# Another order of the first stage's steps and loads in a fused cross-attention and mixture-of-experts block

## The chip, the cores and the metric

The kernel runs on one core of one Trainium2 chip. A core has five engines with instruction queues of their own: TensorE (PE in the profile; PEld is its loading of weights), VectorE (DVE), ScalarE (ACT), GpSimd (POOL) and SyncE (SP), which here issues most of the DMA transfers. The metric is the device time of one execution in microseconds; smaller is better. Before the change the median of three runs was 314.81 us (314.62 to 315.84).

## The reference

The block adds two branches to x (2 x 512 rows of 1024). The first multiplies two matrices that are quantized to 8 bits and back; the second is a mixture of experts with one shared and two chosen experts per row.

```python
def fake_quant(x, scale, zp):
    q = jnp.clip(jnp.round(x / s + z), 0.0, 255.0)
    return (q - z) * s

def _L0_xattn_ref(x1, x2, x1_scale, x1_zp, x2_scale, x2_zp):
    return jnp.matmul(fake_quant(x1, x1_scale, x1_zp), fake_quant(x2, x2_scale, x2_zp))

def _L0_ffn_ref(x, router_w, ...):
    scores = softmax(xt @ router_w + router_b) + router_bias
    # 16 experts in 4 groups: the best 2 of the best 2 groups are chosen, gate holds their scores
    ...
    for each expert:  h = silu(xt @ w1 + b1) * (xt @ w2 + b2);  y += gate * (h @ w3 + b3)
    z = silu(xt @ sw1 + sb1) * (xt @ sw2 + sb2) @ sw3 + sb3       # shared expert, 512 wide
    return y + z

x = x + tanh(g_xattn) * _L0_xattn_ref(_layernorm(x), ctx_4096, ...)
x = x + tanh(g_ffn) * _L0_ffn_ref(_layernorm(x), ...)
```

## The kernel before

The 1024 rows are eight tiles X0 to X7 of 128 rows; tiles 0 to 3 belong to batch 0, 4 to 7 to batch 1. The context of a batch is 1024 x 1024, read as eight tiles c.0 to c.7 of 128 rows.

The kernel has a first stage, in which both quantized products, the second normalization and the first part of the shared expert are worked out, and later stages of dense matmuls (the rest of the shared expert, the router, the chosen experts, the down projections), in which the order of the work is written in loops and lists further down. This change touches the first stage alone. Its order is written out by hand in the string START (line 43): each word is a step, and a line of code (760) calls the function of that name, in that order, under a manual schedule. A step's instructions go to the queue of the engine that it names, so the order of the words is the order on each engine, and an engine that waits holds up everything behind it in its queue. The waits for data and for buffers follow from the tiles that the steps read and write.

The steps, by their letters; t is a row tile, b a batch, k a context tile, h a half of the columns, c a chunk of the shared expert (128 of its 512 columns), i its first or second weight:

- bn, ag (184, 188): statistics of tile t, for the first normalization, on VectorE; each half takes 512 columns.
- qa, qp, qr (193 to 202): variance plus epsilon, the power -1/2 (always on GpSimd), and the scale and offset that join normalization and quantization. qn (206) turns the offset's sign, for ScalarE's form.
- q8 (216, or 214 on ScalarE): tile t to 8-bit numbers. qc (169 on ScalarE, 171 otherwise): minus the zero point, to bf16. qt (227): eight transposes on TensorE. qe (163, 165): the transposed tile from PSUM to SBUF.
- c8 (240, 242) and cc (169, 171): the same two conversions for a context tile.
- mm.t.k (252): two matmuls of 512 columns that add context tile k to tile t's product. The whole sum over k stays in two PSUM banks.
- e (264): X = X + scaled product, with the row sums. sq (273), fm, fc, fa, fr (282 to 298), fn (302): the second normalization. px (307): four transposes; xh and xl (163, 317): the transposed rows as a high and a low part. xc (324): a negated copy for the router, in batch 1.
- wh, wl (163, 165 and 555): the same split for a half of a shared weight. um.c.lo.i.p (564): pass p of three (high x high, high x low, low x high) of chunk c for 256 rows of batch 0; us and ug (571, 574) finish it, ud (331) stores it.
- kb.n (536): n matmuls of zeros, which nobody reads, to keep TensorE at work. xd (328): stores X for the last stage. ld (576): the loads of batch 1's context and of X6 and X7. lw (582): the router's weights. lv (587): both weights of chunk 2; lz: those of chunk 3. pb, bt: the biases, transposed. stage, xx: take buffers. pw (616): the sum of XH and XL for the router, four adds of 128 x 1024 on GpSimd (642). rc (601): constants of the router.

The first loads are not in START, but in LOADS (line 42), issued before it on SP's queue in that order (lines 496 to 507): x.t a row tile, c.k a context tile of batch 0 (c.7 in halves), w.c.i a shared weight, b the biases. X0 is loaded ahead of all, in two halves. Eight transfers are under way at a time: each waits until the eighth before it has landed.

Buffers: six PSUM banks for products (ps_mm) and two for transposes (ps_tr), seven small buffers for the 8-bit and bf16 tiles, 14 of 16 KB per partition (octs) and 17 of 4 KB (slabs). A step that takes a buffer waits until its last reader is done.

After START the rest of the shared expert begins with L364, for batch 1 (from 94.42 us), then the router (L653, from 99.88 us).

Of the kernel before, what the change touches and what calls it, by code (L numbers as in the profile page):

```python
# [42 lines left out]
START = """
bn.0.0 bn.0.1 kb.12 ag.0 qa.0.dve kb.1 bn.1.0 bn.1.1 kb.3 ag.1 qp.0 qr.0.pool qa.1.pool stage.0 kb.2 q8.0.dve.0 bn.3.0
qp.1 bn.3.1 qc.0.act.0 c8.0.0.act.0 ag.3 ld qt.0.0 qr.1.pool qa.3.pool q8.1.dve kb.3 q8.0.dve.1 qp.3 qr.3.pool
qe.0.act.0 c8.0.0.dve.1 kb.3 cc.0.0.pool.0 q8.3.dve qc.1.act cc.0.0.pool.1 c8.0.1.act cc.0.1.act qt.1 qc.0.act.1
qe.1.dve mm.0.0 bn.2.0 qc.3.pool mm.1.0 bn.2.1 ag.2 qt.3 c8.0.3.act c8.0.2.pool qa.2.pool mm.1.1 qe.3.dve mm.0.1 qp.2
cc.0.2.dve c8.0.4.dve qr.2.pool qt.0.1 cc.0.3.act c8.0.5.act cc.0.4.pool mm.3.0 mm.3.1 mm.0.2 mm.1.2 qe.0.act.1 mm.3.2
c8.0.7.act.0 mm.0.3 q8.2.dve mm.1.3 qc.2.dve cc.0.5.pool mm.3.3 c8.0.6.dve mm.1.4 c8.0.7.pool.1 cc.0.6.dve mm.3.4
mm.0.4 cc.0.7.dve.0 qt.2 lw mm.1.5 mm.1.6 mm.1.7.0 cc.0.7.dve.1 qe.2.act e.1.0 mm.0.5 mm.1.7.1 wh.1.1.0.act e.1.1  # L50
mm.0.6 mm.0.7.0 mm.3.5 mm.0.7.1 e.0.0 mm.3.6 e.0.1 sq.1.0 sq.1.1 fm.1.pool fc.1.pool mm.2.0 bn.4.0 fa.1.dve bn.4.1
fm.0.pool sq.0.0 fr.1 fc.0.dve mm.2.1 pb fn.1.0 mm.2.2 mm.2.3 mm.2.4 sq.0.1 fa.0.pool bt wh.1.0.0.act wh.1.1.1.act
fr.0 mm.2.5 px.1.0.m xx.0 xh.1.0.act fn.1.1 xd.1 px.1.1.m xh.1.1.act fn.0.0 fn.0.1 xd.0 wl.1.0.0.pool ag.4 mm.3.7.0
px.0.0 px.0.1 xl.1.0 xl.1.1 xh.0.0.act mm.2.6 xh.0.1.act mm.3.7.1 mm.2.7.1 xl.0.0 mm.2.7.0 wh.1.0.1.act xl.0.1
qa.4.dve wl.1.1.1.pool wl.1.0.1.pool um.1.0.1.0 bn.5.0 qp.4 qr.4.pool bn.5.1 e.2.0 ag.5 wh.0.0.0.act wh.0.0.1.act
um.1.0.0.0 c8.1.1.pool qn.4.dve stage.1 wh.0.1.0.act e.3.0 wh.0.1.1.act c8.1.0.act qa.5.dve q8.4.act um.1.0.0.1
um.1.0.0.2 qp.5 wl.1.1.0.dve qr.5.dve um.1.0.1.1 wl.0.0.1.dve cc.1.0.act um.0.0.0.0 um.0.0.1.0 um.1.0.1.2
wl.0.0.0.pool um.0.0.1.1 lv us.1.0 q8.5.dve um.0.0.0.1 qc.4.act wl.0.1.0.dve c8.1.2.pool qt.4 qc.5.act wl.0.1.1.dve
qe.4.act um.0.0.0.2 qt.5 us.0.0 cc.1.1.pool ug.1.0 ud.1.0 um.0.0.1.2 e.2.1 cc.1.2.act c8.1.5.act c8.1.3.pool qe.5.dve
mm.4.0 mm.5.0 cc.1.3.pool cc.1.5.act c8.1.4.dve ug.0.0 ud.0.0 c8.1.6.dve bn.6.0 cc.1.4.pool mm.4.1 c8.1.7.pool  # L60
cc.1.6.act mm.4.2 sq.2.0 mm.5.1 wh.2.0.0.act cc.1.7.pool bn.6.1 mm.4.3 bn.7.0 bn.7.1 sq.2.1 mm.5.2 mm.4.4 ag.6 ag.7
qa.7.pool wh.2.0.1.dve e.3.1 qp.7 mm.5.3 wl.2.0.1.pool qr.7.dve mm.5.4 qa.6.dve mm.5.5 qn.7.dve q8.7.act mm.4.5
wh.2.1.0.dve qp.6 mm.5.6 qc.7.act mm.4.6 mm.4.7 mm.5.7 um.2.0.0.0 fm.2.pool qr.6.pool wh.2.1.1.dve fc.2.pool fm.3.pool
e.5.0 sq.3.0 fa.2.pool um.2.0.0.1 wl.2.0.0.dve um.2.0.1.0 e.4.0 um.2.0.1.1 qt.7 fc.3.pool sq.3.1 sq.5.0 qe.7.dve
um.2.0.0.2 q8.6.dve e.5.1 mm.7.0 fr.2 mm.7.1 wl.2.1.1.dve mm.7.2 wl.2.1.0.pool mm.7.3 mm.7.4 fa.3.pool mm.7.5 qc.6.act
mm.7.6 fr.3 qt.6 sq.5.1 mm.7.7 fm.5.pool um.2.0.1.2 fc.5.pool fa.5.pool fn.2.0 qe.6.act e.4.1 fn.2.1 xd.2 us.2.0 fr.5
px.2.0.m e.7.0 mm.6.0 fn.3.1 px.2.1 sq.4.0 e.7.1 xh.2.0.act fm.4.pool mm.6.1 mm.6.2 ug.2.0 ud.2.0 sq.7.0 mm.6.3 mm.6.4
mm.6.5 fn.3.0 xd.3 px.3.0.m px.3.1 mm.6.6 sq.4.1 fn.5.1 xh.2.1.act mm.6.7 fm.7.pool xl.2.0 xh.3.0.act xx.1 fn.5.0 xd.5
xh.3.1.act rc fc.4.dve xl.2.1 fa.4.pool sq.7.1 xl.3.0 e.6.0 px.5.1.m sq.6.0 um.2.256.1.0 xl.3.1 um.1.256.0.0 e.6.1
um.2.256.0.0 fm.6.dve fc.7.pool fa.7.pool fc.6.dve fr.7 sq.6.1 fa.6.pool px.5.0 um.1.256.0.1 fn.7.0 xh.5.1.act xc.5.1  # L70
fr.4 um.1.256.0.2 fn.7.1 xd.7 fr.6 fn.4.0 fn.6.1 xh.5.0.act xc.5.0 um.2.256.0.1 um.2.256.0.2 px.7.0.m fn.4.1 xd.4
px.7.1 xl.5.0 um.1.256.1.0 xh.7.1.dve xc.7.1 um.2.256.1.1 xl.7.1 px.4.0 fn.6.0 xd.6 px.6.1 us.2.256 um.2.256.1.2
px.4.1.m xl.5.1 us.1.256 um.0.256.0.0 xh.7.0.dve xc.7.0 ug.2.256 xh.6.1.act xc.6.1 xh.4.1.act xc.4.1 xl.4.1
um.0.256.1.0 um.1.256.1.1 xl.7.0 xh.4.0.dve xc.4.0 xl.4.0 xl.6.1 px.6.0.m um.1.256.1.2 um.0.256.0.1 ug.1.256
xh.6.0.act xc.6.0 xl.6.0 um.0.256.0.2 um.0.256.1.1 um.0.256.1.2 us.0.256 ug.0.256 lz pw ud.2.256 ud.1.256 ud.0.256
"""


# [1138 lines left out]
```

## Time and profile before

| | us |
|---|---|
| median of three runs (lowest, highest) | 314.81 (314.62, 315.84) |
| the profiled execution | 315.13 |
| its span, from the first to the last instruction | 313.0 |
| TensorE busy | 297.2 |
| VectorE busy | 215.2 |
| ScalarE busy | 144.7 |
| GpSimd busy | 97.9 |
| mean granted TensorE clock | 0.994 of full speed |

The lines that follow under the prediction are from the page of this execution and from answers of its trace. The page cuts the span into 40 slices and gives the busy share of each in tenths. A row of the trace's order of time gives start, duration, engine, source line, operation, output and input, and in brackets the time that the engine had been idle and what released it. VectorE and GpSimd rows of one operation differ in length from case to case, since a duration holds the time in which the instruction stood at its engine.

### The profile page before, as it was taken

The numbers are of one execution on the slowest core, as the hardware profiler recorded it, in microseconds if no ns is written. First come the engines' busy times: TensorE is split into PE (matmuls) and PEld (weight loads), VectorE is DVE, ScalarE is ACT, GpSimd is POOL, SyncE is SP. The second block draws the span as 40 slices with busy tenths as digits, with TensorE's granted clock in tenths as the row PEclk, the third lists the DMA queues.
The fourth block names the chain that finished last, engine by engine and source line by source line (L and its number), as shares of the span: only waits on it lengthen the run. The fifth ranks groups of instructions, "written<-read, shape, count | busy, mean of one in ns | idle before, by whom it ended". The sixth has DMA issues, their size and how long they took to land.

```text
span 313.0 us, 4306 instructions
## 1 busy us (share of the span) xinstructions
PE 297.2 (95%) x1536; PEld 235.7 (75%) x1541; DVE 215.2 (69%) x351; ACT 144.7 (46%) x210; POOL 97.9 (31%) x133
## 2 busy tenths in 40 slices
PE   7488799999999999999999999999999999999993
...
GB/s 196 420 385 338 417 355 150 6 2 342 146 17 37 101 201 214 91 138 30 111 167 33 171 1 168 101 66 325 331 294 346 309 221 287 321 89 73 98 101 73
DMA packets 39838, 56.90 MB, mean 182 GB/s; under 512 B 5547, under 2 KB 23027, under 8 KB 39810
## 3 DMA queue, kind: packets, MB, share of 16 engines
...
## 4 chain that ended last, share of the span: by engine, by line
PE 87%; DMA 6%; SPq 5%; DVE 1%; issue 1%; DVEq 0%
PE sp L564 11%; PE sp L364 11%; PE pb L945 11%; PE pa L945 7%; PE pc L945 6%; DMA cr<-in_dram 6%; PE at L252 5%; PE b7B L408 3%; PE b6B L408 3%; PE b5B L408 3%; PE b4B L408 3%; PE b3B L408 3%; PE px L307 2%; PE b7C L408 2%; PE b7A L408 2%; PE b6C L408 2%
## 5 line engine op out<-in xcount | busy, mean ns | idle before, releaser
L252 PE MATMUL at<-cq,qT 128*128 128x512 bf16 x123 | 29.7, 379 | 2.6 <-POOL cq L171 1.4
L252 PEld LDWEIGHTS <-qT 128*128 128x128 bf16 x128 | 12.2, 98 | 15.4 <-issue 2.8
L798 POOL DMA_DIRECT2D xf<-xf x8 | 7.2, 936 | 27.6 <-PE pl L653 14.7
L916 POOL DMA_DIRECT2D rS<-hrouted x6 | 7.3, 1579 | 23.1 <-DMA rS<-hshared 15.4
L564 PE MATMUL sp<-XH,sb 128*128 128x256 f32 x96 | 14.1, 292 | 0.0
L956 DVE SCALAR_TENSOR_TENSOR Y<-pb,tg,Y 128x512 f32<-128x512 f32 x12 | 8.9, 745 | 7.1 <-PE pb L945 5.5
L564 PE MATMUL sp<-XH,sa 128*128 128x256 f32 x96 | 13.7, 287 | 0.0
L317 DVE TENSOR_TENSOR XL<-px,XH 128x512 fp32r<-128x512 f32 x16 | 10.4, 678 | 3.8 <-ACT xf L324 3.8
L956 DVE SCALAR_TENSOR_TENSOR Y<-pc,tg,Y 128x512 f32<-128x512 f32 x8 | 5.9, 749 | 10.0 <-PE pc L945 10.0
L564 PEld LDWEIGHTS sp<-XH,sb 128*128 128x128 f32 x96 | 12.3, 190 | 0.5 <-DVE sb L165 0.2
L564 PEld LDWEIGHTS sp<-XH,sa 128*128 128x128 f32 x96 | 12.3, 191 | 0.1
L273 ACT ACTIVATE xn<-X,s 128x512 f32<-128x512 f32 x16 | 11.4, 716 | 2.1 <-DVE X L264 1.8
L184 DVE BATCH_NORM_STATS2 st<-X 128x6 f32<-128x512 f32 x16 | 10.3, 680 | 2.9 <-DMA X<-in_dram 2.9
L364 PE MATMUL sp<-XH,sb 128*128 128x512 f32 x48 | 12.2, 396 | 0.0
L302 DVE TENSOR_SCALAR xn<-X,nm,d 128x512 f32<-128x512 f32 x16 | 11.2, 726 | 1.4 <-POOL d L298 1.3
L364 PE MATMUL sp<-XH,sa 128*128 128x512 f32 x48 | 11.9, 390 | 0.0
L169 ACT ACTIVATE qx<-q8x,nz 128x1024 bf16<-128x1024 uint8 (+1 forms) x7 | 7.2, 1023 | 10.1 <-DVE q8x L216 10.0
L264 DVE SCALAR_TENSOR_TENSOR X<-at,cx_scale,X 128x512 f32<-128x512 f32 x16 | 11.6, 740 | 0.1
L307 PE MATMUL px<-ident,xn 128*128 128x128 f32 x64 | 9.2, 274 | 1.9 <-DVE xn L302 1.1
L364 PEld LDWEIGHTS sp<-XH,sb 128*128 128x128 f32 x48 | 8.9, 188 | 2.6 <-issue 0.8
L171 POOL TENSOR_SCALAR cq<-q8c,nz 128x1024 bf16<-128x1024 uint8 (+1 forms) x8 | 10.0, 1251 | 1.1 <-DVE q8c L242 0.7
L364 PEld LDWEIGHTS sp<-XH,sa 128*128 128x128 f32 x48 | 8.9, 188 | 1.8
...
## 6 DMA issues: line engine op xcount, KB each, us to landing
...
```

Of the source, the lines that this page charges most:

```text
L184: nc.vector.bn_stats(st_[t][:, h, :], X[t][:, half(h)])
L252: nc.tensor.matmul(acc[t][h], qT[b][:, t % TB, k, :], cq[b][k // KH][:, k % KH, half(h)], start=(k == 0), stop=(k == KD - 1))
L264: nc.vector.scalar_tensor_tensor(xs, acc[t][h], cx_scale, xs, ALU.mult, ALU.add, accum_out=sq_[t][0][:, h : h + 1])
L273: nc.scalar.activation(xn_[t][:, half(h)], X[t][:, half(h)], AF.Square, bias=s[:, h : h + 1], scale=-float(H), accum_out=q[:, h : h + 1],)
L302: nc.vector.tensor_scalar(xn_[t][:, half(h)], X[t][:, half(h)], nm, r, ALU.add, ALU.mult)
L307: nc.tensor.transpose(px_[t, q][:, k, :], xn_[t][:, ts(4 * q + k, P)], ident)
L317: nc.vector.tensor_tensor(XL[b][q][p], px_[t, q], XH[b][q][p].bitcast(F32), ALU.subtract)
L364: nc.tensor.matmul(p, wx[:, k, :], xx[b][k // KH][:, k % KH, cols], start=first and k == 0, stop=last and k == KD - 1,)
L408: nc.tensor.matmul(p, w[:, k, :], x[:, k, :], start=f and k == 0, stop=l and k == KH - 1, skip_group_check=not first,)
L564: nc.tensor.matmul(up_[c, lo, i], w[:, k, :], x[0][k // KH][:, k % KH, lo : lo + 256], start=p == 0 and k == 0, stop=p == 2 and k == KD - 1,)
L945: nc.tensor.matmul(p, x[:, ts(t, P)], w[:, cl], start=first and k == 0 and i == 0, stop=k == KH - 1 and i == 2, skip_group_check=not first,)
L956: nc.vector.scalar_tensor_tensor(X[t][:, cl], p, tgf, X[t][:, cl], ALU.mult, ALU.add)
```

## The change

The text of both strings is replaced. The number of words of START is 430 in both, and its steps are the same but for the engine that a step names and for which steps are cut into halves. No code below the strings changes.

Conversions by engine in START (a half counts 0.5), before and after: context c8 on ScalarE 6 and 12, VectorE 4.5 and 1.5, GpSimd 5.5 and 2.5; context cc on ScalarE 6 and 6, VectorE 3 and 4.5, GpSimd 7 and 5.5; row tiles qc on ScalarE 6 and 2.5, VectorE 1 and 1, GpSimd 1 and 4.5; qe on ScalarE 4 and 2.5, VectorE 4 and 5.5; weights wh on ScalarE 9 and 6, VectorE 3 and 6; wl on VectorE 6 and 4, GpSimd 6 and 8.

In LOADS, x.4 goes ahead of c.7's second half and x.5 right behind it, and w.0.0 becomes the first of the weights. In START, tile 0's whole scale and its first quantized half come ahead of tile 1's statistics; ld comes later in the list and lv, lw and xd change places; the order of um, of mm for batch 1 and of px for the later tiles changes.

The diff, with the first part of START, up to the middle of batch 1's products:

```diff
-LOADS = "x.1 x.3 c.0 c.1 x.2 c.2 c.3 c.4 c.5 c.6 c.7.0 c.7.1 w.1.1 x.4 b w.1.0 w.0.1 x.5 w.0.0"
+LOADS = "x.1 x.3 c.0 c.1 x.2 c.2 c.3 c.4 c.5 c.6 c.7.0 x.4 c.7.1 x.5 w.0.0 w.1.0 w.1.1 b w.0.1"
 START = """
-bn.0.0 bn.0.1 kb.12 ag.0 qa.0.dve kb.1 bn.1.0 bn.1.1 kb.3 ag.1 qp.0 qr.0.pool qa.1.pool stage.0 kb.2 q8.0.dve.0 bn.3.0
-qp.1 bn.3.1 qc.0.act.0 c8.0.0.act.0 ag.3 ld qt.0.0 qr.1.pool qa.3.pool q8.1.dve kb.3 q8.0.dve.1 qp.3 qr.3.pool
-qe.0.act.0 c8.0.0.dve.1 kb.3 cc.0.0.pool.0 q8.3.dve qc.1.act cc.0.0.pool.1 c8.0.1.act cc.0.1.act qt.1 qc.0.act.1
-qe.1.dve mm.0.0 bn.2.0 qc.3.pool mm.1.0 bn.2.1 ag.2 qt.3 c8.0.3.act c8.0.2.pool qa.2.pool mm.1.1 qe.3.dve mm.0.1 qp.2
-cc.0.2.dve c8.0.4.dve qr.2.pool qt.0.1 cc.0.3.act c8.0.5.act cc.0.4.pool mm.3.0 mm.3.1 mm.0.2 mm.1.2 qe.0.act.1 mm.3.2
-c8.0.7.act.0 mm.0.3 q8.2.dve mm.1.3 qc.2.dve cc.0.5.pool mm.3.3 c8.0.6.dve mm.1.4 c8.0.7.pool.1 cc.0.6.dve mm.3.4
-mm.0.4 cc.0.7.dve.0 qt.2 lw mm.1.5 mm.1.6 mm.1.7.0 cc.0.7.dve.1 qe.2.act e.1.0 mm.0.5 mm.1.7.1 wh.1.1.0.act e.1.1
-mm.0.6 mm.0.7.0 mm.3.5 mm.0.7.1 e.0.0 mm.3.6 e.0.1 sq.1.0 sq.1.1 fm.1.pool fc.1.pool mm.2.0 bn.4.0 fa.1.dve bn.4.1
-fm.0.pool sq.0.0 fr.1 fc.0.dve mm.2.1 pb fn.1.0 mm.2.2 mm.2.3 mm.2.4 sq.0.1 fa.0.pool bt wh.1.0.0.act wh.1.1.1.act
-fr.0 mm.2.5 px.1.0.m xx.0 xh.1.0.act fn.1.1 xd.1 px.1.1.m xh.1.1.act fn.0.0 fn.0.1 xd.0 wl.1.0.0.pool ag.4 mm.3.7.0
-px.0.0 px.0.1 xl.1.0 xl.1.1 xh.0.0.act mm.2.6 xh.0.1.act mm.3.7.1 mm.2.7.1 xl.0.0 mm.2.7.0 wh.1.0.1.act xl.0.1
-qa.4.dve wl.1.1.1.pool wl.1.0.1.pool um.1.0.1.0 bn.5.0 qp.4 qr.4.pool bn.5.1 e.2.0 ag.5 wh.0.0.0.act wh.0.0.1.act
-um.1.0.0.0 c8.1.1.pool qn.4.dve stage.1 wh.0.1.0.act e.3.0 wh.0.1.1.act c8.1.0.act qa.5.dve q8.4.act um.1.0.0.1
-um.1.0.0.2 qp.5 wl.1.1.0.dve qr.5.dve um.1.0.1.1 wl.0.0.1.dve cc.1.0.act um.0.0.0.0 um.0.0.1.0 um.1.0.1.2
-wl.0.0.0.pool um.0.0.1.1 lv us.1.0 q8.5.dve um.0.0.0.1 qc.4.act wl.0.1.0.dve c8.1.2.pool qt.4 qc.5.act wl.0.1.1.dve
-qe.4.act um.0.0.0.2 qt.5 us.0.0 cc.1.1.pool ug.1.0 ud.1.0 um.0.0.1.2 e.2.1 cc.1.2.act c8.1.5.act c8.1.3.pool qe.5.dve
-mm.4.0 mm.5.0 cc.1.3.pool cc.1.5.act c8.1.4.dve ug.0.0 ud.0.0 c8.1.6.dve bn.6.0 cc.1.4.pool mm.4.1 c8.1.7.pool
-cc.1.6.act mm.4.2 sq.2.0 mm.5.1 wh.2.0.0.act cc.1.7.pool bn.6.1 mm.4.3 bn.7.0 bn.7.1 sq.2.1 mm.5.2 mm.4.4 ag.6 ag.7
-qa.7.pool wh.2.0.1.dve e.3.1 qp.7 mm.5.3 wl.2.0.1.pool qr.7.dve mm.5.4 qa.6.dve mm.5.5 qn.7.dve q8.7.act mm.4.5
-wh.2.1.0.dve qp.6 mm.5.6 qc.7.act mm.4.6 mm.4.7 mm.5.7 um.2.0.0.0 fm.2.pool qr.6.pool wh.2.1.1.dve fc.2.pool fm.3.pool
...
+bn.0.0 bn.0.1 ag.0 qa.0.dve qp.0 qr.0.dve q8.0.dve.0 bn.1.0 kb.12 qc.0.pool.0 bn.1.1 stage.0 kb.1 kb.3 q8.0.dve.1 ag.1
+qt.0.0 qe.0.act.0 qa.1.pool bn.3.0 bn.3.1 qc.0.act.1 kb.2 c8.0.0.act.0 c8.0.0.act.1 ag.3 c8.0.1.act qp.1 qa.3.pool
+qp.3 cc.0.1.act xx.0 qr.1.dve cc.0.0.dve.0 c8.0.2.act kb.3 q8.1.dve qr.3.pool cc.0.0.dve.1 mm.0.0 qc.1.dve qt.1
+q8.3.dve qc.3.pool c8.0.3.act kb.3 mm.0.1 qe.1.dve bn.2.0 mm.1.0 bn.2.1 qt.0.1 ag.2 qt.3 qe.3.dve qa.2.dve cc.0.2.pool
+c8.0.4.act qe.0.dve.1 cc.0.4.act mm.1.1 mm.1.2 cc.0.3.pool mm.0.2 c8.0.5.dve cc.0.5.dve mm.3.0 mm.1.3 qp.2 mm.0.3
+qr.2.dve c8.0.7.dve.0 mm.3.1 q8.2.dve cc.0.7.dve.0 mm.1.4 mm.1.5 bn.4.0 mm.0.4 mm.3.2 c8.0.6.act qc.2.pool mm.3.3
+bn.4.1 c8.0.7.pool.1 cc.0.6.act ag.4 mm.1.6 mm.3.4 qt.2 bn.5.0 cc.0.7.pool.1 mm.1.7.0 mm.0.5 mm.0.6 mm.3.5 mm.1.7.1
+qa.4.pool e.1.0 mm.3.6 qe.2.act bn.5.1 qp.4 e.1.1 wh.0.0.0.act mm.0.7.0 sq.1.0 mm.0.7.1 e.0.0 sq.1.1 e.0.1 ag.5
+wl.0.0.0.pool fm.1.pool fc.1.pool mm.2.0 fa.1.dve fr.1 mm.2.1 sq.0.0 mm.2.2 fm.0.dve wh.1.0.0.dve sq.0.1 mm.2.3 mm.2.4
+fc.0.dve fn.1.1 pb fa.0.dve wh.1.1.0.dve mm.2.5 qr.4.pool mm.2.6 px.1.1.m bt wh.0.0.1.act fn.1.0 fr.0 mm.3.7.1
+qa.5.dve ld qp.5 xh.1.1.act mm.2.7.0 px.1.0.m wl.1.0.0.pool fn.0.0 fn.0.1 px.0.0 xl.1.1 px.0.1 mm.3.7.0 e.2.0
+xh.1.0.act mm.2.7.1 xh.0.0.act xh.0.1.act qn.4.dve wh.1.0.1.act wh.1.1.1.dve e.2.1 xl.1.0 wh.0.1.0.act wh.0.1.1.act
+qr.5.pool um.0.0.0.0 um.1.0.0.0 um.0.0.1.0 wl.1.1.1.pool q8.4.act c8.1.1.act xl.0.0 xl.0.1 um.1.0.1.0 wl.1.1.0.pool
+c8.1.5.act q8.5.dve qc.5.pool wl.0.1.1.pool qc.4.act c8.1.2.act wl.1.0.1.dve um.0.0.1.1 lv um.1.0.0.1 wl.0.1.0.dve
+um.0.0.0.1 sq.2.0 qt.5 c8.1.0.pool um.1.0.0.2 e.3.0 wl.0.0.1.dve e.3.1 c8.1.7.act bn.6.0 stage.1 um.0.0.0.2 qe.5.dve
+cc.1.1.act us.1.0 um.0.0.1.2 cc.1.0.pool us.0.0 qt.4 c8.1.4.act um.1.0.1.1 xd.1 qe.4.dve xd.0 um.1.0.1.2 mm.4.0 mm.4.1
+mm.5.0 bn.6.1 mm.5.1 cc.1.2.pool fm.3.pool bn.7.0 mm.4.2 c8.1.3.pool bn.7.1 ag.6 wh.2.1.0.dve wh.2.0.0.dve
+wh.2.0.1.act cc.1.3.act ug.0.0 ug.1.0 c8.1.6.act qa.6.dve wh.2.1.1.dve cc.1.4.pool mm.5.2 ag.7 cc.1.5.dve fm.2.pool
+cc.1.6.act qa.7.dve mm.4.3 sq.3.0 fc.2.pool wl.2.0.0.pool sq.2.1 sq.3.1 mm.5.3 qp.6 cc.1.7.dve mm.4.4 fa.2.dve
+um.2.0.0.0 mm.5.4 mm.5.5 mm.4.5 mm.4.6 qr.6.dve qp.7 qr.7.pool fc.3.pool q8.6.dve mm.5.6 qn.7.dve mm.5.7 fa.3.dve fr.2
+um.2.0.0.1 e.5.0 fn.2.0 fn.2.1 um.2.0.1.0 q8.7.act qc.6.pool mm.4.7 qt.6 um.2.0.1.1 e.4.0 xd.3 qc.7.act qt.7 qe.6.dve
+mm.6.0 e.5.1 mm.6.1 mm.6.2 qe.7.act mm.6.3 mm.6.4 mm.6.5 sq.4.0 sq.5.0 px.2.1 fm.5.dve fr.3 e.4.1 xh.2.1.act fn.3.0
...
```

More of the change, by code (lines that the diff above doesn't have):

```diff
@@ L62 @@
-qa.7.pool wh.2.0.1.dve e.3.1 qp.7 mm.5.3 wl.2.0.1.pool qr.7.dve mm.5.4 qa.6.dve mm.5.5 qn.7.dve q8.7.act mm.4.5
-wh.2.1.0.dve qp.6 mm.5.6 qc.7.act mm.4.6 mm.4.7 mm.5.7 um.2.0.0.0 fm.2.pool qr.6.pool wh.2.1.1.dve fc.2.pool fm.3.pool
-e.5.0 sq.3.0 fa.2.pool um.2.0.0.1 wl.2.0.0.dve um.2.0.1.0 e.4.0 um.2.0.1.1 qt.7 fc.3.pool sq.3.1 sq.5.0 qe.7.dve
-um.2.0.0.2 q8.6.dve e.5.1 mm.7.0 fr.2 mm.7.1 wl.2.1.1.dve mm.7.2 wl.2.1.0.pool mm.7.3 mm.7.4 fa.3.pool mm.7.5 qc.6.act
-mm.7.6 fr.3 qt.6 sq.5.1 mm.7.7 fm.5.pool um.2.0.1.2 fc.5.pool fa.5.pool fn.2.0 qe.6.act e.4.1 fn.2.1 xd.2 us.2.0 fr.5
@@ L67 @@
[L67 to L75, printed above, removed]
+bn.0.0 bn.0.1 ag.0 qa.0.dve qp.0 qr.0.dve q8.0.dve.0 bn.1.0 kb.12 qc.0.pool.0 bn.1.1 stage.0 kb.1 kb.3 q8.0.dve.1 ag.1
```

10 lines of the change are left out of this document (added).

## The prediction, made before the changed kernel ran

> **What bounds the kernel now.** I read the page first (shares and slices), then TensorE's waits, then the order of time in the first 51 us, then stretches of 1 us for the clock.
>
> ```profile
> span 313.0 us, 4306 instructions
> PE 297.2 (95%) x1536; PEld 235.7 (75%) x1541; DVE 215.2 (69%) x351; ACT 144.7 (46%) x210; POOL 97.9 (31%) x133
> PE   7488799999999999999999999999999999999993
> ```
>
> TensorE (PE) is busy 297.2 of 313.0 us; all its holes but the last lie in the first five slices of 7.8 us. After that nothing but its own work sets the time, so the change can win at most holes before 38 us, and loses if it opens new ones later.
>
> ```profile
> PE pq L227 <- ACT qx L169: 4.4, 1, 4.4
> PE at L252 <- POOL cq L171: 1.4, 3, 0.6
> PE px L307 <- DVE xn L302: 1.1, 1, 1.1
> PE at L252 <- DVE cq L171: 0.9, 1, 0.9
> PE px L307 <- DVE mv L188: 0.8, 1, 0.8
> PE pq L227 <- POOL qx L171: 0.4, 1, 0.4
> ```
>
> All waits of TensorE after its start (total, times, longest): 9.0 us. A first one for tile 0's quantized half, then conversions, then the normalized rows before the transposes of L307.
>
> ```profile
> 9.03 1.29 DVE L184 BATCH_NORM_STATS2 st<-X 128x6 f32<-128x512 f32 x2 [2.45 <-DMA X<-in_dram]
> 10.47 0.49 DVE L216 TENSOR_SCALAR q8x<-X,qa,qb 128x512 uint8<-128x512 f32 x1
> 11.00 0.72 ACT L169 ACTIVATE qx<-q8x,nz 128x512 bf16<-128x512 uint8 x1 [6.93 <-DVE q8x L216]
> ...
> 33.44 1.27 POOL L555 TENSOR_TENSOR sa<-sa1r,sa 128x512 fp32r<-128x512 f32 x1
> 33.51 2.89 DVE L302 TENSOR_SCALAR xn<-X,nm,d 128x512 f32<-128x512 f32 x2 [0.45 <-POOL d L298]
> ...
> 37.90 1.30 PE L564 MATMUL sp<-XH,sb 128*128 128x256 f32 x8
> ...
> 50.84 6.85 PE L252 MATMUL at<-cq,qT 128*128 128x512 bf16 x31
> ```
>
> Start, duration, engine, line. Tile 0's scale was ready at 8.0 (L202 on GpSimd, 7.61 + 0.39), but its first half (L216) stands behind tile 1's statistics, which wait for tile 1's load until 9.03. The two L302 at 33.51 took 2.89 where the pair before took 1.00: each ran only when GpSimd's L555 had ended. From 37.90 the shared experts' matmuls (um) run without a hole; mm.4 follows at 50.84.
>
> ```profile
> 12.00:13.00 1.00, 1.00 (x7) 0.58 1.00 410
> 13.00:14.00 1.00, 1.00 (x4) 0.50 1.06 434
> 14.00:15.00 1.00, 1.00 (x7) 0.50 0.99 406
> 15.00:16.00 1.00, 0.59 (x6) 0.72 1.06 434
> 16.00:17.00 1.00, 0.56 (x2) 1.00 1.01 414
> ```
>
> Stretch, sum, TensorE's busy time, granted clock, DMA share, GB/s: half a clock from about 12.0 to 15.4, after the hole of 4.4 us.
>
> **The change, part by part.** No instruction of the main path is added or removed in kind; they change engine and order. I walk the new order (as the built instructions stand, with the producers they wait for) with durations of the trace.
>
> *Tile 0 alone.* The power on GpSimd ends at 7.23. The two scale operations now follow on VectorE (0.15 and 0.27, as L201 and L202 take there at best, 7.75), the first half of q8 0.49 (8.25), its centring on GpSimd 0.57 (the half cq of L171 that released TensorE at 16.14, once VectorE's L216 was out at 15.6): 8.9 instead of 11.72. Transposes 9.4, copy by ScalarE 0.56: 10.0. Nothing follows at once, for mm.0.0 needs the first context tile.
>
> *VectorE* from tile 1's landing at 9.03: statistics 1.29, tile 0's second half 0.49, aggregate 0.2, tile 3's statistics 1.28 and aggregate 0.2 (12.5), tile 1's scale 0.4, half cq 0.45, q8.1 0.81, half cq 0.45, qc.1 0.76: 15.4. So mm.0.0 runs at 13.4 and 14.8 instead of 16.14, but tile 1's transposes come at 15.5, 0.9 later than now (14.56).
>
> *ScalarE* takes six of eight context conversions of batch 0 instead of four: from 10.9, qc 0.72, c8.0 in halves 2 x 0.70, c8.1 1.24 and cc.1 1.06 (spacings of 14.41 to 16.72) make 15.3; c8.2, c8.3, c8.4 19.0, cc.4 20.1, then c8.6 behind its load. The loads keep just ahead: SP's issues at 15.26 and 16.47, each held until an earlier transfer landed, put c.2 at 15.2 and c.3 at 16.4; at 1.25 each c.6 lands at 20.3, so c8.6 is 21.6 and cc.6 22.6. GpSimd: qc.3 17.4, cc.2 18.5, cc.3 19.6 (1.11 each, L171). VectorE again: qe.1, tile 2's statistics, qe.3, half qe.0, c8.5 and cc.5 21.6, halves c8.7 and cc.7 24.0. Now the same tiles 4 to 7 are ready at 23.6, 25.2, 26.5 and 27.7; then at 20.1, 21.6, 22.6 and 24.0 (its second half by GpSimd, after qc.2, 26.6). This is the real gain. x.4 goes ahead of c.7.1 and costs that half 1.25 us: 22.8, hidden, as GpSimd takes it at 24.7; if GpSimd were early, it would wait there.
>
> *TensorE* from 15.5: 28 transposes at 0.056 (0.45 for eight), three fillers, 58 matmuls at 0.215 (16 in 3.62 is 0.226; 6.50 for 32 from 50.84 is 0.203) is 14.9: 30.4 without a wait. Waits: qe.3 for mm.3.0, qc.2, mm.1.7.1 and e.1.1's bank, about 0.9: 31.3. The clock is not shown for a hole of 2.2 us (6.7 to 8.9) with patches of work after it: bounds are no throttle (0) and a half clock over 15.5 to 19, costing about 1.2. I take 1.2, since the trace throttled after 4.4 us of little work, and here 7 to 15 is thin too: 32.5. [...]
>
> Then e, sq, fm, fa, fr as now; on VectorE fa.1, fm.0, one weight cast and fn.1 in turn: fn.1.1 32.5, fn.1.0 33.6, fn.0.0 34.2, fn.0.1 34.7. Transposes and ScalarE's copy (0.45 + 0.58) end at 35.8; um starts at 35.6 on its first half. Against 37.90: minus 2.3.
>
> *Behind it.* 12 um at 0.96 and two qt take 12.5: mm.4 at 48.1 (now 12.94). VectorE was busy 39.65 of the 42.1 us from 37.9 to 80. It loses two c8 (3.0), tile 5's statistics (1.3) and weight remainders (about 1.0), and gains two cc, a qe and casts (some 2.7 in all): 2.6 less, so the earlier start fits. One order is tight: c8.1.3 on GpSimd stands behind cc.1.0, cc.1.2 and fm.3 (46.7, 47.8, 48.6), runs to 50.2 under VectorE's casts, and cc.1.3 on ScalarE ends at 51.3 where mm.4.3 is due at 50.6: plus 0.65 (0 to 2).
>
> *Queues.* On SP the eight loads of batch 1 keep their place in bytes. w.2's second half now stands ahead of x_after and waits for px.1.0 (33.1); the router's weights stand behind ug.1.0 (about 51). Their readers are at 79.72 (GpSimd's L642, done 89.36) and 99.88 (L653): cover of 10 and 40 us, beyond which each us late is a us lost. On GpSimd, rc (0.8) goes behind L642, ahead of its DMAs after 103: nothing.
>
> Sum: 313.0 - 2.3 + 0.65 = 311.35 span. The profiled execution took 315.13, 2.13 more than its span, and lies 0.32 above the median of 314.81. 315.13 - 1.65 = 313.5; against the median **313.2**.
>
> **Rivals.**
> 1. *No throttle, no late wait.* Minus 1.2 and minus 0.65 more: 311.3. For it: the thin stretches are filled with work. Against: mm.4.3 is late in my walk in any case.
> 2. *The gain is spent before um.* Waits between engines that I count at 0.05 to 0.1 stretch, and fn.0 meets L555 again (wl.1.0.0 starts about 33.4): plus 1.9, as the 2.89 against 1.00 now. 314.81 + 0.25 = 315.1 with a late wait, 314.4 without: no change.
> 3. *VectorE and GpSimd take turns* (slower). Between 39 and 53 VectorE has q8.5, three weight remainders, three casts and two cc against GpSimd's L555, L242 and L171. The trace's pairs: q8 0.81 and 1.61, L555 0.68 and 1.47, cast 0.38 and, by the same waiting, an estimate of 0.8, L171 0.76 and 1.31. If all meet, 0.8 + 2.4 + 1.2 + 1.1 = 5.5 us on VectorE. It decides once qe.4 (47.1 in my walk, due 48.1) and cc.1.5 (53.0, due 54) are over 1 us late: 4.5 lost, 314.81 - 2.3 + 4.5 = 317.0. For it: the 2.89 above. Against: GpSimd is busy only 10.28 of the 12.94 us from 37.9 to 50.84, and the L555 on VectorE at 47.52 took 0.68. [...]
>
> That it does nothing is excluded: the built order differs on every engine.
>
> **How the numbers follow.** Forecast 0.45 (its own range 312.3 to 314.2), rival 1 0.15, rival 2 0.18, rival 3 0.22, of which 0.1 beyond 317. Measured "no change" is within 0.5%, 1.57 us. Faster: rival 1 and the 0.65 of the forecast's range that lies below 313.24, 0.15 + 0.29 = 0.44; slower 0.22; same the rest, 0.16 + 0.18 = 0.34. The range goes from 311.3 to 317.0, about 0.1 left out on each side.
>
> **What would show it.** First L227 at about 9, first L252 below 14; c8 and cc of tile 6 done by 23; first L564 near 35.6; a wait of TensorE for cc.1.3 near 51. Wrong if L564 starts after 37, or if waits of TensorE after 40 add up to over 2 us.

## The result, and the profile after the change

The changed kernel takes 311.33 us (median of four executions, 310.69 to 312.81); the kernel before, on the same chip, 315.32 (314.62 to 316.22). The ratio is 0.988, with a 95% interval of 0.983 to 0.992. All medians here are of executions in the fast state: two of kernel K's ten (314.84 and 433.46) and two of the kernel before (319.41 and 380.59), clearly slower and two of them at a far lower granted clock (0.66 and 0.75), are left out. The profiled execution took 311.35 us. Its page, with the granted clock below TensorE's slices:

```profile
span 309.4 us, 4287 instructions
PE 297.0 (96%) x1536; PEld 235.9 (76%) x1541; DVE 208.0 (67%) x365; ACT 145.0 (47%) x206; POOL 95.4 (31%) x123
PE   8499999999999999999999999999999999999992
PEclk9889999999999999999999999999999999999998
```

TensorE has the same work (297.0 against 297.2 us) in a span shorter by 3.6 us. The holes are now in the first two slices. All waits of TensorE behind its first instruction (total, times, longest):

```profile
PE at L252 <- ACT q8c L240: 2.4, 1, 2.4
PE pq L227 <- POOL qx L171: 1.9, 2, 1.4
...
PE at L252 <- DVE cq L171: 0.7, 1, 0.7
```

These are 5.0 us (the wait left out is for the fillers' zeros, 1.4 in both kernels), against 9.0 before: 4.0 less, about the whole gain. The order of time (start, duration, engine, line; in brackets the idle time and its releaser):

```profile
7.71 0.55 DVE L216 TENSOR_SCALAR q8x<-X,qa,qb 128x512 uint8<-128x512 f32 x1
8.36 0.69 POOL L171 TENSOR_SCALAR qx<-q8x,nz 128x512 bf16<-128x512 uint8 x1 [1.19 <-DVE q8x L216]
9.10 0.40 PE L227 MATMUL pq<-ident_b,qx 128*128 128x128 bf16 x4 [1.36 <-POOL qx L171]
...
13.01 0.38 PE L252 MATMUL at<-cq,qT 128*128 128x512 bf16 x1 [2.44 <-ACT q8c L240]
...
14.13 0.58 PE L252 MATMUL at<-cq,qT 128*128 128x512 bf16 x1 [0.74 <-DVE cq L171]
14.80 1.03 PE L227 MATMUL pq<-ident_b,qx 128*128 128x128 bf16 x8
15.63 1.48 PE L536 MATMUL pz<-zero 128*128 128x512 bf16 x3
16.91 1.18 PE L252 MATMUL at<-cq,qT 128*128 128x512 bf16 x4
...
31.93 1.00 DVE L302 TENSOR_SCALAR xn<-X,nm,d 128x512 f32<-128x512 f32 x2
...
32.52 1.55 POOL L555 TENSOR_TENSOR sa<-sa1r,sa 128x512 fp32r<-128x512 f32 x1
...
33.92 2.19 PE L564 MATMUL sp<-XH,sa 128*128 128x256 f32 x16
...
46.55 4.06 PE L252 MATMUL at<-cq,qT 128*128 128x512 bf16 x17
...
57.05 0.62 PE L227 MATMUL pq<-ident_b,qx 128*128 128x128 bf16 x8 [0.54 <-POOL qx L171]
```

Tile 0 starts at 9.10 instead of 11.78. Tile 1's transposes are at 14.80; in the kernel before they were here:

```profile
14.56 1.04 PE L227 MATMUL pq<-ident_b,qx 128*128 128x128 bf16 x8
```

So nothing is won up to them: TensorE waited 4.4 us ahead of them before and 4.5 now, and they come 5.81 us behind tile 1's statistics (8.99), against 5.53 before (9.03). What went are the waits behind them, 4.6 before and 0.5 now. From 14.80 to 33.92 the trace names no wait of TensorE. The pair of L302 that took 2.89 us takes 1.00, and now GpSimd's L555 is the one that is stretched (1.55, where most take 1.27 to 1.30). The first um is at 33.92 instead of 37.90, which is 3.98 earlier, and the difference stays to the end but for 0.4 us. Behind it stands one wait, 0.54 at 57.05. The clock in stretches of 1 us (stretch, sum, TensorE's busy time, granted clock, DMA share, GB/s):

```profile
13.00:14.00 1.00, 0.38 (x1) 0.90 1.01 414
14.00:15.00 1.00, 0.79 (x4) 0.50 1.03 422
15.00:16.00 1.00, 1.00 (x9) 0.50 1.02 418
16.00:17.00 1.00, 1.00 (x4) 0.50 1.02 418
17.00:18.00 1.00, 1.00 (x7) 0.89 1.03 416
```

Half a clock from 13.8 to 17.2: once again 3.4 us, later than before (12.15 to 15.57).

### The profile page after: what moved, and what is told of

It reads as the page before. It is cut to its first block, busy times and chain, and to the rows that moved or that the text cites. A ratio compares the mean times of both kernels' runs of the same rounds, so it can differ in the third digit from the quotient of the medians.

```text
span 309.4 us, 4287 instructions
## 1 busy us (share of the span) xinstructions
PE 297.0 (96%) x1536; PEld 235.9 (76%) x1541; DVE 208.0 (67%) x365; ACT 145.0 (47%) x206; POOL 95.4 (31%) x123
## 4 chain that ended last, share of the span: by engine, by line
PE 85%; POOL 5%; DVE 4%; DMA 2%; ACT 1%; issue 1%; SPq 0%; POOLq 0%
PE sp L364 11%; PE pb L945 11%; PE sp L564 9%; PE pa L945 7%; PE pc L945 6%; PE at L252 3%; PE b7B L408 3%; PE b6B L408 3%; PE b5B L408 3%; PE b4B L408 3%; PE b3B L408 3%; PE px L307 2%; DMA X<-in_dram 2%; PE b7C L408 2%; PE b6C L408 2%; PE b6A L408 2%
## 5 line engine op out<-in xcount | busy, mean ns | idle before, releaser
L240 ACT ACTIVATE q8c<-cr,sc_in,rs 128x1024 uint8<-128x1024 f32 (+1 forms) x13 | 15.0, 1169 | 1.2 <-DMA cr<-in_dram 1.1
L916 POOL DMA_DIRECT2D rS<-hrouted x6 | 7.3, 1578 | 22.2 <-DMA rS<-hshared 15.5
L564 PE MATMUL sp<-XH,sb 128*128 128x256 f32 x96 | 13.3, 286 | 0.0
L184 DVE BATCH_NORM_STATS2 st<-X 128x6 f32<-128x512 f32 x16 | 10.3, 678 | 2.9 <-DMA X<-in_dram 2.9
L163 ACT CAST XH<-px 128x512 fp32r<-128x512 f32 x12 | 6.9, 593 | 7.9 <-PE px L307 7.8
L536 PE MATMUL pz<-zero 128*128 128x512 bf16 x24 | 9.1, 550 | 1.4 <-DVE zero L529 1.4
L642 POOL TENSOR_TENSOR xf<-XH,XL 128x1024 f32<-128x1024 f32 x4 | 9.4, 2394 | 0.0
```

Source lines behind the costliest of these rows:

```text
L184: nc.vector.bn_stats(st_[t][:, h, :], X[t][:, half(h)])
L240: nc.scalar.activation(out, src, AF.Identity, bias=z2c, scale=rs2)
L564: nc.tensor.matmul(up_[c, lo, i], w[:, k, :], x[0][k // KH][:, k % KH, lo : lo + 256], start=p == 0 and k == 0, stop=p == 2 and k == KD - 1,)
L642: eng.tensor_tensor(x, XH[b][i // 2][:, ts(i % 2, 2)].bitcast(F32), XL[b][i // 2][:, ts(i % 2, 2)].bitcast(F32), ALU.add)
```

## The experiments

All kernels compute the whole block. Two columns come from the profiled execution: "um" is the time from tile 1's statistics (the first L184 behind tile 0's) to the first um, so that the first loads, which do not land at the same time in every execution, drop out; "half clock" is taken from stretches of 0.25 us, up to the first um. A ratio is to the kernel before in the same series on the same chip (medians 315.05 to 315.42).

| kernel | median us | ratio to before [95%] | um | half clock |
|---|---|---|---|---|
| before | 315.32 | | 28.87 | 12.15-15.57 |
| changed | 311.33 | 0.988 [0.983, 0.992] | 24.93 | 13.80-17.21 |
| A old START, new LOADS | 314.90 | 0.999 [0.995, 1.002] | 28.92 | 11.56-14.98 |
| B new START, old LOADS | 315.02 | 0.998 [0.995, 1.001] | 29.52 | 14.44-17.84, 31.50-34.91 |
| C new up to um, old behind | 311.35 | 0.986 [0.978, 0.993] | 25.47 | 14.77-18.18 |
| D old, tile 0 first | 315.34 | 0.999 [0.996, 1.003] | 28.61 | 13.78-20.60 |
| E new, tile 0 behind | 313.07 | 0.989 [0.984, 0.995] | 28.08 | 11.13-21.37 |
| F new, old engines | 319.60 | 1.015 [1.007, 1.023] | 33.40 | 9.57-19.81, 30.06-33.47 |
| G new, L555 earlier | 310.47 | 0.985 [0.979, 0.991] | 25.18 | 9.16-12.57 |
| H old, L555 later | 315.89 | 1.001 [0.998, 1.005] | 26.78 | 12.42-19.25 |
| I new, holes filled | 310.52 | 0.985 [0.982, 0.988] | 24.27 | none |
| J as I, less three | 309.75 | 0.984 [0.981, 0.988] | 24.31 | none |
| K new, fewer fillers | 311.68 | 0.989 [0.986, 0.991] | 24.93 | 9.66-16.48 |
| L as J, tile 6 on ScalarE | 310.23 | 0.984 [0.980, 0.987] | 25.62 | 16.29-19.70 |

**A and B: the loads or the order?** One string of each kernel.

```diff
-LOADS = "x.1 x.3 c.0 c.1 x.2 c.2 c.3 c.4 c.5 c.6 c.7.0 c.7.1 w.1.1 x.4 b w.1.0 w.0.1 x.5 w.0.0"
+LOADS = "x.1 x.3 c.0 c.1 x.2 c.2 c.3 c.4 c.5 c.6 c.7.0 x.4 c.7.1 x.5 w.0.0 w.1.0 w.1.1 b w.0.1"
```

The edit of A to the kernel before:

> The old START with the new LOADS. My theory: the loads by themselves bring nothing, they only fit the new order. w.1.1 then lands some 6 us later, near 29, and ScalarE's cast of it stands ahead of tile 1's squares (28.65 before): the squares come 1 to 1.5 us late, um starts at 38.5 to 39.5 instead of 37.90, the time is 315.5 to 317 against 315.3 for the kernel before. Rival, that the order of the loads is the gain: um at 34 to 35, 311 to 312.

B is this edit undone in the changed kernel:

> The new START with the old LOADS. My theory: the new order needs its loads. X5 then lands near 31, and tile 5's statistics on VectorE stand ahead of the residual of tile 1 (25.50 in the changed kernel), so all behind is about 5 us late: um at 38 to 39.5, 315 to 317. Rival, that the loads do not matter and START alone brings the gain: um at 34, 311 to 312.

Neither is told from the kernel before. In A the loss I expected did not come: the cast waited 1.84 us for w.1.1, but the squares behind it came only 0.4 us later against tile 1's residual, and um not at all. B went as expected. Two rows of B, where the new order meets loads that come late:

```profile
28.45 0.69 DVE L184 BATCH_NORM_STATS2 st<-X 128x6 f32<-128x512 f32 x1 [2.87 <-DMA X<-in_dram]
...
30.32 0.62 ACT L163 CAST sa<-sa0r 128x512 fp32r<-128x512 f32 x1 [3.82 <-DMA sa0r<-in_dram]
```

VectorE stands at tile 5's statistics with tile 1's residual behind them; TensorE waits for that residual (2.7 us in two waits), and behind this hole the clock is halved once more, from 31.50 to 34.91. START needs its LOADS; LOADS alone bring nothing.

**C: is the order behind um needed?** The head of the changed kernel, and every later step as before:

```diff
-qr.5.pool um.0.0.0.0 um.1.0.0.0 um.0.0.1.0 wl.1.1.1.pool q8.4.act c8.1.1.act xl.0.0 xl.0.1 um.1.0.1.0 wl.1.1.0.pool
+qr.5.pool lw xd.1 xd.0 xl.0.0 xl.0.1 wl.1.1.1.pool wl.1.0.1.pool um.1.0.1.0 um.1.0.0.0 c8.1.1.pool stage.1 e.3.0
...
```

> The new loads and the new START up to its first um; all steps behind it, with their engines, in the order of the kernel before. My theory: the gain lies ahead of um, so um starts at 33.9 as in the changed kernel and the time is 311.0 to 312.3 (at most 1 us of new waits, since batch 1's context lands no earlier than now). Rival, that the new order behind um is needed to keep the gain: um at 33.9 too, but waits of TensorE between 36 and 60 that add up to 2 us or more, 313.3 to 315.

Tile 1's transposes and the first um in C:

```profile
14.29 0.63 PE L227 MATMUL pq<-ident_b,qx 128*128 128x128 bf16 x8 [0.29 <-DVE qx L171]
...
33.95 1.53 PE L564 MATMUL sp<-XH,sb 128*128 128x256 f32 x8
```

No wait of TensorE behind 14.3 us, 311.35 us: the gain lies ahead of um, and of the rest of the new order nothing can be measured. Up to um, C and the changed kernel have the same steps, and yet the column um has 25.47 and 24.93: half a microsecond there can come from where the half clock falls (see I).

**D and E: tile 0 alone at first.** D puts it into the kernel before (its conversion of tile 0's first half leaves ScalarE, and qt.0.0 moves up with it; the next line, which loses both, is not shown):

```diff
-bn.0.0 bn.0.1 kb.12 ag.0 qa.0.dve kb.1 bn.1.0 bn.1.1 kb.3 ag.1 qp.0 qr.0.pool qa.1.pool stage.0 kb.2 q8.0.dve.0 bn.3.0
+bn.0.0 bn.0.1 kb.12 ag.0 qa.0.dve kb.1 qp.0 qr.0.dve q8.0.dve.0 bn.1.0 qc.0.pool.0 bn.1.1 kb.3 ag.1 qt.0.0 qa.1.pool stage.0 kb.2 bn.3.0
```

> The kernel before with one thing of the change: tile 0's scale (on VectorE) and its first quantized half ahead of tile 1's statistics, that half centred by GpSimd, its transposes moved up. My theory: TensorE's wait of 4.4 us goes from the head to the first context matmul, which still waits for GpSimd's conversion (14.86 + 0.95 before); the sum is 0 to 0.8 us gained, um at 37.1 to 37.9, 314.5 to 315.3 against 315.3. Rival, that the 4.4 us at tile 0 were the loss and go with it: um at 34 to 35.5, 311 to 313.

E takes it out of the changed kernel:

```diff
-bn.0.0 bn.0.1 ag.0 qa.0.dve qp.0 qr.0.dve q8.0.dve.0 bn.1.0 kb.12 qc.0.pool.0 bn.1.1 stage.0 kb.1 kb.3 q8.0.dve.1 ag.1
+bn.0.0 bn.0.1 ag.0 qa.0.dve qp.0 qr.0.dve bn.1.0 kb.12 bn.1.1 stage.0 kb.1 kb.3 ag.1 q8.0.dve.0 qc.0.pool.0 q8.0.dve.1
```

> The changed kernel with one step put back: tile 0's first quantized half on VectorE behind tile 1's statistics again, all else as in the changed kernel. My theory: ScalarE's whole list of conversions hangs on tile 0's copy, so it runs about 1.9 us later, and VectorE, whose first conversion waits for it, too; tile 1's transposes at about 16.7 instead of 14.80; um at 35.4 to 36.0, 312.8 to 313.5 against 311.3. Rival, that it is the conversions' engines and not tile 0 that bring the gain: um at 33.9 to 34.4, 311.3 to 311.8.

D gained nothing that the time shows: the wait of 4.4 us became 1.5, a new one of 2.3 came at tile 1, and the half clock lasted twice as long. E lost 1.7 us by the medians, but its interval and the changed kernel's overlap, so the times alone do not tell the two apart; the traces do. ScalarE, VectorE and TensorE in E:

```profile
12.56 0.58 ACT L163 COPY qT<-pq 128x512 bf16<-128x512 bf16 x1 [8.49 <-PE pq L227]
...
14.50 0.49 DVE L171 TENSOR_SCALAR cq<-q8c,nz 128x512 bf16<-128x512 uint8 x1 [1.15 <-ACT q8c L240]
...
16.83 1.04 PE L227 MATMUL pq<-ident_b,qx 128*128 128x128 bf16 x8
```

The half tile is late, so ScalarE's copy (9.54 in the changed kernel), its conversions, VectorE behind them and tile 1's transposes are late in turn. Against tile 1's statistics the transposes lost 2.11 us, where 1.9 was expected; um lost 3.15. The other 1.04 came behind the transposes, where the clock was still halved for 4.5 us (to 21.37), against 2.4 in the changed kernel. So tile 0 first is worth something only where ScalarE's conversions hang on it, as in the new order, and not by the hole that it closes.

**F: the engines.** The changed kernel with batch 0's conversions on the old engines; shown are only the words that change (c8.0.2 also goes behind qc.3):

```diff
-c8.0.0.act.1 cc.0.0.dve.0 cc.0.0.dve.1 c8.0.2.act cc.0.2.pool c8.0.4.act cc.0.4.act cc.0.3.pool
+c8.0.0.dve.1 cc.0.0.pool.0 cc.0.0.pool.1 c8.0.2.pool cc.0.2.dve c8.0.4.dve cc.0.4.pool cc.0.3.act
-c8.0.5.dve cc.0.5.dve c8.0.7.dve.0 c8.0.6.act cc.0.6.act cc.0.7.pool.1
+c8.0.5.act cc.0.5.pool c8.0.7.act.0 c8.0.6.dve cc.0.6.dve cc.0.7.dve.1
```

> The changed kernel with tile 0 first, but batch 0's context converted by the engines of the kernel before. My theory: GpSimd and VectorE then set the order again (first context product near 15.5 to 16 instead of 13.01, tiles 4 to 7 ready about 2 us later), TensorE waits for conversions 2 to 3 us more, um at 35.4 to 36.5, 312.8 to 314.0. Rival, that tile 0's early start alone brings it: um at 33.9 to 34.4, 311.3 to 311.8.

The sign was right, the size was not: 8.3 us slower than the changed kernel, and slower than the kernel before. GpSimd, VectorE and TensorE in F:

```profile
23.02 2.21 POOL L171 TENSOR_SCALAR cq<-q8c,nz 128x1024 bf16<-128x1024 uint8 x2 [4.33 <-DVE q8c L242]
...
25.80 0.16 DVE L201 TENSOR_TENSOR qa<-r,rs 128x1 f32<-128x1 f32 x1 [2.54 <-POOL r L197]
...
29.56 0.73 DVE L171 TENSOR_SCALAR cq<-q8c,nz 128x1024 bf16<-128x1024 uint8 x1
...
30.34 1.87 PE L252 MATMUL at<-cq,qT 128*128 128x512 bf16 x4 [3.16 <-DVE cq L171]
```

GpSimd waits 4.33 us for VectorE's c8.4, then centres two tiles, and only then raises tile 2's power, for which VectorE waits 2.54 us with tile 6's conversion behind it. Behind the hole that this makes in TensorE's work the clock is halved again, from 30.06 to 33.47. I had priced each conversion by itself; what decides is what stands behind it in its queue. An engine and a place in the order are one choice, so F shows that the new engines are needed for the new order, not what they would be worth alone.

**G and H: where GpSimd's L555 meets VectorE's L302.** G swaps two neighbours on GpSimd in the changed kernel, as in the kernel before, where L555 followed the power of tile 0's variance at once:

```diff
-qa.5.dve ld qp.5 xh.1.1.act mm.2.7.0 px.1.0.m wl.1.0.0.pool fn.0.0 fn.0.1 px.0.0 xl.1.1 px.0.1 mm.3.7.0 e.2.0
+qa.5.dve ld xh.1.1.act mm.2.7.0 px.1.0.m wl.1.0.0.pool qp.5 fn.0.0 fn.0.1 px.0.0 xl.1.1 px.0.1 mm.3.7.0 e.2.0
```

> The changed kernel with two neighbours on GpSimd swapped: the weight remainder (L555) ahead of tile 5's power (L197), not behind it, so that it starts within 0.1 us of VectorE's last two L302, as in the kernel before. If the remainder holds VectorE up there: the two L302 take 2.4 to 2.9 us instead of 1.00, um starts at 35.3 to 35.8 instead of 33.92, 312.7 to 313.2 against 311.3. Rival, that the 2.89 of the kernel before came from something else than the order of the two starts: no change, um at 33.9, 311.3.

Three engines in G:

```profile
30.70 1.27 POOL L555 TENSOR_TENSOR sa<-sa1r,sa 128x512 fp32r<-128x512 f32 x1
...
30.83 1.88 DVE L302 TENSOR_SCALAR xn<-X,nm,d 128x512 f32<-128x512 f32 x2
...
32.39 1.08 PE L307 MATMUL px<-ident,xn 128*128 128x128 f32 x8 [0.93 <-DVE xn L302]
```

L555 starts 0.13 us ahead, the pair takes 1.88 instead of 1.00, and TensorE waits 0.93: the effect is there, at about half the size I gave it. The times do not show it (310.32 to 312.76 against 310.69 to 312.81). In G's profile the half clock fell on 9.16 to 12.57, where TensorE had only tile 0's transposes, fillers and holes, so that it cost little and made up for most of the meeting: against I, below, which has no meeting and no half clock, um is 0.91 late, against the changed kernel 0.25.

H takes the meeting out of the kernel before (only the parts of the lines that differ are shown):

```diff
-px.1.0.m xx.0 xh.1.0.act fn.1.1 xd.1 px.1.1.m xh.1.1.act fn.0.0 fn.0.1 xd.0 wl.1.0.0.pool ag.4 mm.3.7.0
+px.1.0.m xx.0 xh.1.0.act fn.1.1 xd.1 px.1.1.m xh.1.1.act fn.0.0 fn.0.1 xd.0 ag.4 mm.3.7.0
...
-qa.4.dve wl.1.1.1.pool wl.1.0.1.pool um.1.0.1.0 bn.5.0 qp.4 qr.4.pool bn.5.1
+qa.4.dve wl.1.0.1.pool wl.1.0.0.pool um.1.0.1.0 bn.5.0 qp.4 qr.4.pool wl.1.1.1.pool bn.5.1
```

> The kernel before with two weight remainders (L555) of GpSimd moved behind a third one that waits for ScalarE, so that none runs beside VectorE's last two L302. If their meeting was worth the 1.1 + 0.8 us that TensorE waited there: um at 35.8 to 36.4 instead of 37.90, 313.2 to 314.0 against 315.2 (0.3 may be lost again where a um waits for the later remainder). Rival, that these waits only pass to the next producer: um at 37.4 to 37.9, 314.7 to 315.3.

VectorE's pair and two stretches of TensorE in H, in order of time, and then its clock from 50 to 52 us (stretch, sum, TensorE's busy time, granted clock, DMA share, GB/s):

```profile
32.69 1.00 DVE L302 TENSOR_SCALAR xn<-X,nm,d 128x512 f32<-128x512 f32 x2 [0.45 <-POOL d L298]
...
35.19 1.30 PE L564 MATMUL sp<-XH,sb 128*128 128x256 f32 x8
...
48.76 0.62 PE L227 MATMUL pq<-ident_b,qx 128*128 128x128 bf16 x8 [1.99 <-ACT qx L169]
```

```profile
50.00:52.00 2.00, 2.00 (x8) 0.50 0.16 55
```

The pair took 1.00 and um came 2.09 us earlier, as the first theory said; the time is no shorter than before, as the rival said. The remainders that moved, which were done by 36.1 before, now run between um's start and tile 5's power on GpSimd; that power comes at 42.39 (42.09 before, although um now starts 2.71 us earlier), tile 5's transposes wait 1.99 us, and after that hole the clock is halved once more, over the product of batch 1. So what was won ahead of um is lost behind it: from um to the end of the span H takes 278.5 us, the kernel before 275.1. The changed kernel has tile 4's scale ready ahead of um and tile 5's just behind, and keeps the gain.

**I, J and K: the clock.** I fills TensorE's two holes in the changed kernel with matmuls of zeros; J also drops the three behind tile 1; K drops the five in the second hole. The counts of the six kb words, in their order:

```diff
-kb.12 kb.1 kb.3 kb.2 kb.3 kb.3
+kb.12 kb.1 kb.8 kb.2 kb.11 kb.3
```

> The changed kernel with 13 more matmuls of zeros: 5 ahead of tile 0's transposes and 8 ahead of the first context product, in TensorE's two holes. My theory: the half clock (13.9 to 17.1 in the changed kernel) answers to those holes, so it stays away; the stream that started at 16.91 starts at 15.3 to 15.7, is then held by GpSimd's half of tile 3 (about 17.1), um at 32.5 to 33.1 instead of 33.92, 309.9 to 310.6 against 311.3. Rival, that the half clock does not answer to the holes: it falls somewhere all the same, and the 8 fillers at half clock delay the first context product by up to 2 us: 311.3 to 313.

```diff
-kb.12 kb.1 kb.8 kb.2 kb.11 kb.3
+kb.12 kb.1 kb.8 kb.2 kb.11
```

> As the kernel with 13 more matmuls of zeros, and without the three that stand behind tile 1's transposes (15.63 to 16.91 in the changed kernel). My theory: those three lie on the path only while the clock is halved; with a full clock the stream waits for conversions anyway, so 0 to 0.6 us less than the kernel with all of them: 309.5 to 310.4. Rival, that they carry the clock over: the half clock comes back, 310.5 to 312.

```diff
-kb.12 kb.1 kb.3 kb.2 kb.3 kb.3
+kb.12 kb.1 kb.3 kb.3
```

> The changed kernel without the five matmuls of zeros behind tile 0's transposes (9.3 to 10.6). My theory: with one long thin stretch from 7.7 to 14 the half clock lasts two or three times 3.4 us instead of once, um at 34.8 to 36, 312.2 to 313.5 against 311.3. Rival, that fillers there are without effect: 311.3.

TensorE in I:

```profile
14.27 0.62 PE L227 MATMUL pq<-ident_b,qx 128*128 128x128 bf16 x8 [0.29 <-DVE qx L171]
...
15.38 1.22 PE L252 MATMUL at<-cq,qT 128*128 128x512 bf16 x4
...
32.73 2.19 PE L564 MATMUL sp<-XH,sa 128*128 128x256 f32 x16
```

No stretch of I is below full clock up to 306 us, near the span's end. The stream starts at 15.38 instead of 16.91, um at 32.73 instead of 33.92; of these 1.19 us 0.53 are tile 1's earlier statistics (8.46 instead of 8.99). The mean granted clock of all six executions of I is 0.996 to 1.000, of four of the changed kernel 0.990 to 0.993, of K 0.983 to 0.987 (6.82 us of half clock, twice 3.41, as expected). So between these kernels the half clock went with the holes. The loss of 0.9 to 2.2 us that I expected of K did not come: its time is not told from the changed kernel's (0.35 more at the median), and its half clock lies at 9.66 to 16.48, mostly over a hole and fillers. What a half clock costs depends on what it falls on. From tile 1's transposes to um I takes 18.46 us and the changed kernel 19.12, with no wait named behind the transposes in either: 0.66 for the half clock. C, whose half clock lies later against the same steps, takes 19.66: 1.20. L, below, against J makes 1.31 (19.81 and 18.50). J's three fillers less bring 0.8 us at the median, with intervals that overlap; in the traces the two have the same um (24.27 and 24.31).

**L: the late wait.** J with tile 6's centring on ScalarE:

```diff
-um.2.0.0.1 e.5.0 fn.2.0 fn.2.1 um.2.0.1.0 q8.7.act qc.6.pool mm.4.7 qt.6 um.2.0.1.1 e.4.0 xd.3 qc.7.act qt.7 qe.6.dve
+um.2.0.0.1 e.5.0 fn.2.0 fn.2.1 um.2.0.1.0 qc.6.act q8.7.act mm.4.7 qt.6 um.2.0.1.1 e.4.0 xd.3 qc.7.act qt.7 qe.6.dve
```

> The kernel with the holes filled and without the three matmuls of zeros behind tile 1, in which tile 6's centring goes from GpSimd to ScalarE, ahead of tile 7's quantization. In that kernel TensorE still waits 0.41 us for tile 6 at 55.1. My theory: that wait goes, and tile 7's conversions, 0.5 us later on ScalarE, end within 0.1 us of their transposes: 309.2 to 309.7 against 309.75 without this step. Rival, that the wait only passes to tile 7: 309.7 to 310.2.

TensorE at tile 6's transposes in L:

```profile
56.59 0.61 PE L227 MATMUL pq<-ident_b,qx 128*128 128x128 bf16 x8
```

The wait is gone (nothing in brackets), and nothing takes its place at tile 7: 274.4 us from um to the end of the span, 275.1 in J. But this profile has a half clock at 16.29 to 19.70, over the stream, and um 1.3 us later than J. Its clock is 0.991 here and 0.996 to 1.000 in the other five executions, so by the clock it came once in six; TensorE was busy 53% of the 3.41 us ahead of it (12.88 to 16.29), but why it came is not shown, since J has the same fillers and none in its profile. The median, 310.23, shows no gain over J. I, J and L have lower medians than the changed kernel, by 0.8 to 1.6 us; but their intervals overlap with its, and which is best they leave open too.

## Why the prediction was right in sign, and less than half in size

Forecast was 313.2 us, 0.5% faster; it is 311.33, 1.2% faster, 0.03 us inside the lower end of the range (311.3). That end was put there for a rival that did not hold, so that the time lies inside is luck. By its steps:

- *Tile 0 alone*: 8.9, 9.4 and 10.0 were forecast for the half tile, its transposes and the copy; 9.05, 9.10 (to 9.50) and 10.13 came. Right.
- *VectorE*: tile 1's transposes at 15.5; they came at 14.80. I had added up durations, but most of these instructions start 0.08 to 0.09 us before the one ahead ends (L216 at 12.88 lasts 0.81, the next starts at 13.60). Over the chain from 8.99 to 14.74 that is 0.6 of the 0.7 us.
- *TensorE*: the waits of 0.9 that I had put to tile 3's copy, tile 2's centring, the second half of c.7 and a bank did not come (tile 2's centring ended at 24.32 and its transposes ran at 24.64 without a wait; c.7's second half was ready at 25.86, forecast 26.6). The conversions of context tiles 4 to 7 were as early as forecast (cc of tile 6 at 22.69, forecast 22.6): what I called the real gain was there, and the waits for conversions behind tile 1 are gone.
- *Clock*: 1.2 us was taken, for a half clock from 15.5 to 19. It came from 13.80 to 17.21, 1.7 us earlier, and cost 0.66 by I, since part of it fell on a hole and on fillers; 1.20 in C is what I had taken. Every half clock in the table lasted 3.4, 6.8 or 10.2 us, and the first of each run began at another time, from 9.16 us (G) to 16.29 (L).
- *um*: 35.6 forecast, 33.92 measured. This is the term that was mis-sized: minus 2.3 in the sum, minus 3.98 in the trace. Of the 1.7 between them, 0.7 is the earlier start, 0.9 the waits and 0.5 the clock; 0.5 goes back, since without waits and half clock the stretch takes 18.46 (I), where my sum has 18.0.
- *Behind it*: plus 0.65 for a wait at mm.4.3. It did not come there; 0.54 came at tile 6's transposes, for the same kind of reason (a conversion on GpSimd behind other work). Wrong in place, and right in size by luck. In I, where um is earlier, 0.26 did come at mm.4.3 (at 48.39, for ScalarE's cc).

*Rivals.* "No throttle, no late wait" gave 311.3, which is the time measured, but not its reason: both came. "The gain is spent before um" fell in the changed kernel, since tile 5's power stands between tile 0's and L555, 0.5 us that let L302 start first; G shows that without it TensorE waits 0.93. "VectorE and GpSimd take turns" did not decide: VectorE's casts, remainders and centrings behind um kept their lengths (0.42, 0.68 to 0.85, 0.74), while GpSimd's were stretched (tile 5's centring 2.01, where most take 1.12), and GpSimd had the room. Which of the two is longer went with which started first: with L555 0.13 ahead of L302 in G the pair took 1.88, with L555 0.59 behind in the changed kernel L555 itself took 1.55. In the kernel before, each of the two L302 ended 0.28 us behind the L555 beside it (34.99 and 34.71, 36.39 and 36.11), while one takes 0.54 by itself; that it ran only when that L555 had ended, as I wrote, these rows do not show.

What the parts are worth alone does not add up to the 3.94 us of um: the meeting of L555 and L302 was worth 2.09 in the old order (H, whose half clock was twice as long), tile 0's place 2.11 at tile 1's transposes in the new one (E), and next to nothing in the old (D). How much of the rest the engines bring by themselves stays open, since F changes their waits on each other too.
